# Attention over sixteen batches: the norm, queries, keys and values of batches 4 to 9 computed during batches 0 to 2 and passed through DRAM

## The chip, the cores and the metric

The kernel runs on one core of one Trainium2 chip. The metric is device time in microseconds (us) of one execution, as the median of several. The engines of a core are named as the profile names them: PE (TensorE, matmuls), PEld (the weight loads that run beside PE), DVE (VectorE), ACT (ScalarE), POOL (GpSimd) and SP (SyncE, which here only issues DMAs). Each engine takes its own instructions strictly in order.

## The reference

Two layers, each a conditioning block followed by a feed-forward block, over x of 16 batches x 256 tokens x 256 features, all in float32. Only the last block is touched: attention with 16 heads of 16 features, then a mixture of 8 experts of which each token takes 2.

```python
x = x + _L0_ffn_ref(_L0_cond_ref(x, ...), ...)
y = _L1_cond_ref(x, ...)              # a recurrence over the 256 tokens
x = x + _L1_ffn_ref(y, ...)

def _L1_ffn_ref(x, ln1_g, ln1_b, w_qkv, b_qkv, w_o, b_o, ...):
    h = _layernorm(x, ln1_g, ln1_b)
    q, k, v = jnp.split(h @ w_qkv + b_qkv, 3, axis=-1)
    ...
    scores = jnp.einsum('bqhd,bkhd->bhqk', q, k) / np.sqrt(DK)
    attn = jax.nn.softmax(scores, axis=-1)
    o = jnp.einsum('bhqk,bkhd->bqhd', attn, v).reshape(B, S, D)
    x = x + o @ w_o + b_o
    h = _layernorm(x, ln2_g, ln2_b).reshape(B * S, D)
    topv, topi = jax.lax.top_k(h @ gate_w + gate_b, TOPK)
    ...
    hid = jax.nn.relu(jnp.einsum('td,edf->etf', h, W1) + b1[:, None, :])
    out_e = jnp.einsum('etf,efd->etd', hid, W2) + b2[:, None, :]
    return x + jnp.einsum('etd,te->td', out_e, ew).reshape(B, S, D)
```

What matters for the change: in attention a batch needs nothing from another batch, so the norm, queries, keys and values of any batch can be computed as soon as the recurrence has ended. The experts of a token can be chosen only when attention of its batch has ended.

## The kernel before

The first layer and the recurrence of the second take the time to 2383 us. They leave the recurrence's output, in layout [128 partitions, 2 halves of the features, tokens], in a DRAM tensor `zd`; batch 0 of it also stays on chip in `z0`. The change lies in the stage behind that: attention, batch after batch, with the experts' work interleaved.

Per batch there are three generators, that is functions whose `yield` marks a place where other work may be put between:

- `front(b)` loads z of the batch after (`load_z`), normalizes z of batch b (`normed`: matmuls with a matrix of 1/256 for the mean, L1207, and the variance, L1216; DVE subtracts, takes the reciprocal, scales and shifts, L1209 and L1219 to L1222; POOL squares, L1211; ACT takes the square root, L1218), then makes queries and keys (L1241, evacuated by ACT at L1244 into the tile `qk`) and values (L1252, evacuated by DVE at L1254 into one of two buffers `vbuf`).
- `heads(b)` is the attention itself. For each of four groups of heads (`QC` = 4) it computes the scores once to find each row's largest (L1277, DVE at L1284), moves the queries by it (L1289, L1290), computes the scores again (L1277), takes the exponential (ACT, L1296), and at the end of each half multiplies by the values (L1305, evacuated at L1306 and L1307).
- `ends(b)` divides by the row sums, projects (L1339), adds the residual, normalizes again, picks the experts and scatters each token's row to its expert's place in DRAM (L1330 to L1468).

The experts' work is a fourth generator, `experts()`: for each of 71 tiles of 128 rows it loads rows and weights (L1486 to L1495), transposes (L1501), and does two matrix products, L1513 with W1 and L1526 with W2. W2 of all experts sits in one on-chip tile `mw2` (64 KB a partition, 8 MB in all), loaded by eight DMAs of 1 MB at the start of the stage (L1117).

`drive` puts them together. During batch b it steps through `heads(b)`, and between its places takes steps of `ends(b - 1)`, `front(b + 1)` and the experts. How many tiles belong to a batch follows from how many are certain to be full: none in batches 0 to 2, the first three steps of one (its loads) in batch 3, and then three or four a batch until batch 15 (`allowed`, `planned`). What is left runs alone after attention, from 3341 us.

The text's order is not the engines' order. A scheduler sorts the instructions of each engine by when it expects them to be ready, so work of neighbouring batches overlaps, and a DMA may be issued far ahead of the text. A wait that turns out longer than expected then blocks what stands behind it on that engine.

PSUM, the matmuls' output memory, is full: two buffers of pool `pmm` (handed out by `mm()`, and used by every small product of `front`, `heads` and `ends`), four of `psc` for the scores, two of `pg` for the experts' tiles.

The loop of the stage, with the number of steps that each side work gets in a batch:

```python
steps(front(0))
for b in range(B):
    sides = []
    if b:
        sides.append((ends(b - 1), 9))
    if b + 1 < B:
        sides.append((front(b + 1), 6))
    drive(heads(b), sides, planned(b - 1), planned(b), NPL)
drive(ends(B - 1), [], planned(B - 1), allowed(B - 1), 16)
```

Of the kernel before, what the change touches and what calls it, by code (L numbers as in the profile page):

```python
# [8 lines left out]
F32 = mybir.dt.float32  # L9
# [8 lines left out]
P = 128  # L18
B, T, D = 16, 256, 256
N = B * T  # L20
KC = D // P
E = 8
# [8 lines left out]
AH, DK = 16, 16  # L31
DFF = 1024
NF = DFF // P
# [6 lines left out]
def bc(ap, axis, n):  # L40

    a = ap.unsqueeze(axis)
    shape = list(a.shape)
    shape[axis] = n
    return a.to_broadcast(shape)


def steps(gen, n=None):

    while n is None or n > 0:  # L50
        if next(gen, gen) is gen:
            return
        n = None if n is None else n - 1
# [108 lines left out]
def adaln_ffn_kernel(ctx: ExitStack, tc: tile.TileContext, i: dict, out: bass.AP):  # L162
    nc = tc.nc
# [74 lines left out]
    with (  # L238
# [402 lines left out]
    zd = dram.tile([P, KC, B, T], F32, name="zd")  # L641
    late.close()
    with tc.tile_pool(name="cw", bufs=1) as cw:
# [8 lines left out]
        dram2 = ctx.enter_context(tc.tile_pool(name="dram2", bufs=1, space=DRAM))  # L652
# [7 lines left out]
        QC = AH * 32 // P  # L660
# [18 lines left out]
        with (  # L679
# [276 lines left out]
            def new_w():  # L956
                return cx.tile([P, NC, P], F32, name="wts")
# [6 lines left out]
            early = new_w()  # L964
            w = new_w()
# [37 lines left out]
            g = dt.tile([P, 5, KC * CW], F32, name="g")  # L1003
# [21 lines left out]
            for u in range(NCH + 1):  # L1025
# [20 lines left out]
                for q in range(NQ):  # L1046
                    if u < NCH:
                        steps(dense, 1)
                    if u + 1 < NCH:
# [26 lines left out]
    QC = AH * 32 // P  # L1076
    HC = AH // QC
    QP = QC // 2
    NTT = T // P
    I32 = mybir.dt.int32  # L1080
    final = ctx.enter_context(ExitStack())
    with (
# [5 lines left out]
        fx = attn.enter_context(tc.tile_pool(name="fx", bufs=2))  # L1088
# [5 lines left out]
        zs = {0: z0}  # L1094

        def load_z(b):
            zs[b] = fx.tile([P, KC, T], F32, name="z", bufs=3)
            nc.sync.dma_start(out=zs[b], in_=zd[:, :, b])
# [9 lines left out]
        for m in range(2 * HC):  # L1108
            to, at = slice(m * DK, (m + 1) * DK), slice(m % HC * 32, m % HC * 32 + DK)
# [3 lines left out]
        wg = load("wg", [P, KC, E], fl)  # L1113
        bg = load("bg", [P, E], fl)
        mw2 = ew.tile([P, E, NF, D], F32, name="mw2")
        for e in range(E):
            nc.sync.dma_start(out=mw2[:, e], in_=i["mw2"][:, e])  # L1117

        ones_d = fl.tile([P, P], F32, name="ones_d")
        nc.vector.memset(ones_d, 1.0 / D)  # L1120
# [34 lines left out]
        vbuf = [fl.tile([P, NTT, AH, 32], F32, name=f"v{n}") for n in range(2)]  # L1155
# [41 lines left out]
        now = {"count": count, "full": full, "tiles": tiles}  # L1197
        sent = []

        def mm():  # L1200
            return pmm.tile([P, NTT, T], F32, name="mm", tag="mm")

        def normed(x, which, out):

            mean = mm()[:, 0]
            for k in range(KC):
                nc.tensor.matmul(mean, ones_d, x[:, k], start=(k == 0), stop=(k == KC - 1))  # L1207
            h = fx.tile([P, KC, T], F32, name=f"h{which}", bufs=2 - which)
            nc.vector.tensor_tensor(h, x, bc(mean, 1, KC), ALU.subtract)  # L1209
            sq = fx.tile([P, KC, T], F32, name="sq", bufs=1)  # L1210
            nc.gpsimd.tensor_tensor(sq, h, h, ALU.mult)  # L1211
            out.append(h)
            yield
            var = mm()[:, 0]
            for k in range(KC):
                nc.tensor.matmul(var, ones_d, sq[:, k], start=(k == 0), stop=(k == KC - 1))  # L1216
            rs = fx.tile([P, T], F32, name="rs", bufs=1)
            nc.scalar.activation(rs, var, AF.Sqrt, bias=eps)  # L1218
            nc.vector.reciprocal(rs, rs)  # L1219
            nc.vector.tensor_tensor(h, h, bc(rs, 1, KC), ALU.mult)  # L1220
            for k in range(KC):
                nc.vector.tensor_scalar(  # L1222
                    h[:, k], h[:, k], lnw[:, 2 * which, k : k + 1], lnw[:, 2 * which + 1, k : k + 1], ALU.mult, ALU.add
                )
            yield

        qks, vs, outs = {}, {}, {}

        def front(b):

            if b + 1 < B and b > 0:
                load_z(b + 1)
            o = []
            yield from normed(zs[b], 0, o)
            hn = o[0]
            qk = qks[b] = fx.tile([P, 2, QC, T], F32, name="qk")
            for w in range(2):
                pq = mm()
                for c in range(QP):
                    for k in range(KC):  # L1240
                        nc.tensor.matmul(pq[:, c], wqk[:, w, k, c * P : (c + 1) * P], hn[:, k], start=(k == 0), stop=(k == KC - 1))  # L1241
                for c in range(QP):
                    for r in range(2):
                        nc.scalar.activation(  # L1244
                            qk[:, w, 2 * c + r], pq[:, c], AF.Identity, bias=bias[:, w, c, r : r + 1], scale=keep[:, w, r : r + 1]
                        )
                    yield
            v = vs[b] = vbuf[b % 2]
            pv = mm()
            for t in range(NTT):  # L1250
                for k in range(KC):
                    nc.tensor.matmul(pv[:, t], hn[:, k, t * P : (t + 1) * P], wv[:, k], start=(k == 0), stop=(k == KC - 1))  # L1252
            for t in range(NTT):
                nc.vector.tensor_tensor(  # L1254
                    v[:, t].rearrange("p (m a) (h r) -> p m (a h) r", a=2, h=2)[:, :, 0:4:3],
                    pv[:, t].rearrange("p (m a r) -> p m a r", a=2, r=DK),
                    bv.rearrange("p (m a r) -> p m a r", a=2, r=DK),
                    ALU.add,
                )
            yield  # L1260

        def rows(j):
# [60 lines left out]
        def ends(b):  # L1323
# [20 lines left out]
            yield  # L1344
            o = []
            yield from normed(z, 1, o)
            nc.gpsimd.tensor_tensor(x, x, z, ALU.add)
            nc.scalar.dma_start(out=x3d[:, :, b * T : (b + 1) * T], in_=x)
# [204 lines left out]
        def go(to):  # L1553

            if to > state["gone"]:
                steps(moe, to - state["gone"])
                state["gone"] = to

        def allowed(m):

            return max(0, min(NTL, m * 2 * T // P - E + 1))

        def planned(b):

            return min(allowed(b - 1), 5 + max(0, b - 4) * 40 // 11)

        def drive(main, sides, tiles_from, tiles_to, places):

            a, z = tiles_from * PIECES, tiles_to * PIECES
            for k in range(places):  # L1570
                steps(main, 1)
                for s, n in sides:
                    steps(s, (k + 1) * n // places - k * n // places)
                go(a + (z - a) * (k + 1) // places)
            steps(main)
            for s, _ in sides:
                steps(s)

        NPL = 2 * QC + 1
        steps(front(0))  # L1580
        for b in range(B):
            sides = []
            if b:
                sides.append((ends(b - 1), 9))
            if b + 1 < B:
                sides.append((front(b + 1), 6))
            drive(heads(b), sides, planned(b - 1), planned(b), NPL)
        drive(ends(B - 1), [], planned(B - 1), allowed(B - 1), 16)
        attn.close()
        pools["first"] = final.enter_context(tc.tile_pool(name="ep2", bufs=2, space=PSUM))  # L1590
# [7 lines left out]
        for c in range(NBLK):  # L1598
            t = jx.tile([P, KC, TBLK], F32, name=f"base{c}")
# [93 lines left out]
```

## Time and profile before

| what | us |
|---|---|
| median of 3 runs (3614.8 to 3624.22) | 3615.62 |
| the profiled execution, own time | 3609.16 |
| its span, first to last instruction | 3607.4 |
| recurrence ends (last step's DVE instruction, L951) | 2383.3 |
| front of batch 0 on PE | 2384.0 to 2401.5 |
| heads of batches 0 to 15 | 2401.5 to 3340.6 |
| experts' rest and the output | 3340.6 to 3607.4 |

The end of a batch is taken here as the start of its second copy at L1306, which frees the last product of its heads. These copies start at 2441.0, 2494.3, 2543.2, 2593.0 (batches 0 to 3), 2658.3, 2711.8, 2777.4, 2832.4, 2900.1 (batches 4 to 8), and 2965.0, 3019.1, 3085.1, 3151.4, 3208.2, 3275.6, 3340.6. So batches 1 to 3 take 53.3, 48.9 and 49.8 us, and from batch 4 on a batch takes 53 to 57 us with three tiles of experts and 65 to 68 us with four.

In tables of stretches of time the columns are, for each stretch: its length, then busy us and (instructions) of PE, PEld, DVE, ACT and POOL, the TensorE clock that the throttle granted as a share of full speed, the mean busy share of the 16 DMA engines, and GB/s. In a timeline each line is a group of equal instructions: start, length, engine, line of the kernel, operation, output and inputs, count; in brackets the engine's idle time before it and what ended it. PE records overlap a little, because matmuls are pipelined, so the time that a group holds PE is taken from its start to the start of the next.

### The profile page before, as it was taken

The numbers are of one execution on the slowest core, as the hardware profiler recorded it, in microseconds if no ns is written. First come the engines' busy times: TensorE is split into PE (matmuls) and PEld (weight loads), VectorE is DVE, ScalarE is ACT, GpSimd is POOL, SyncE is SP. The second block draws the span as 40 slices with busy tenths as digits, with TensorE's granted clock in tenths as the row PEclk, the third lists the DMA queues.
The fourth block names the chain that finished last, engine by engine and source line by source line (L and its number), as shares of the span: only waits on it lengthen the run. The fifth ranks groups of instructions, "written<-read, shape, count | busy, mean of one in ns | idle before, by whom it ended". The sixth has DMA issues, their size and how long they took to land.

```text
span 3607.4 us, 72831 instructions
## 1 busy us (share of the span) xinstructions
PE 3373.3 (94%) x26776; PEld 2564.6 (71%) x26776; DVE 2277.7 (63%) x7358; ACT 1492.2 (41%) x3701; POOL 686.0 (19%) x1164
## 2 busy tenths in 40 slices
PE   8899969999999999999999999969999999999896
PEld 4377456777777777777777777735677777777796
DVE  3333477988788887878788787435555556564323
ACT  1133135555454544545454554334444434443221
POOL 4545220000000100000010100101222222222221
PEclk9999989999999999999999999968999999999997
DMA  6333441011111111011111111130223333332566
GB/s 213 125 108 104 146 73 29 18 36 22 36 19 33 24 35 33 20 36 22 36 19 33 28 28 31 24 123 21 70 92 114 104 119 103 117 102 97 195 216 222
DMA packets 422255, 272.78 MB, mean 76 GB/s; under 512 B 304720, under 2 KB 381136, under 8 KB 411024
## 3 DMA queue, kind: packets, MB, share of 16 engines
q1 hardware_dynamic: 397504, 207.95, 20.9%
q0 software_dynamic: 13344, 36.60, 2.7%
q10 hardware_dynamic: 11056, 23.60, 1.9%
q8 instruction: 216, 3.54, 0.4%
q14 instruction: 135, 1.11, 0.1%
HBM read 191.62 MB, written 76.44 MB: 74 GB/s over the span
## 4 chain that ended last, share of the span: by engine, by line
PE 73%; DVE 10%; issue 5%; DMA 4%; ACT 4%; POOL 2%; SPq 1%; ACTq 0%; DVEq 0%; POOLq 0%
PE acc L865 13%; PE po L839 9%; PE gp L933 7%; PE wp L822 7%; PE g L1526 6%; PE g L1513 5%; PE sc L1277 3%; PE bp L889 3%; PE sp L736 3%; PE ph L529 2%; PE mm L1305 2%; PE py L543 2%; DVE i L747 2%; DVE s L746 1%; PE mm L1241 1%
## 5 line engine op out<-in xcount | busy, mean ns | idle before, releaser
L839 PEld LDWEIGHTS po<-yt,kin 128*128 128x128 f32 x3840 | 459.1, 191 | 104.4 <-issue 103.5
L865 PEld LDWEIGHTS acc<-ge,kout 128*128 128x128 f32 x3968 | 467.0, 192 | 86.1 <-issue 42.4
L865 PE MATMUL acc<-ge,kout 128*128 128x128 f32 x3968 | 505.5, 280 | 3.2 <-DVE ge L862 1.7
L839 PE MATMUL po<-yt,kin 128*128 128x128 f32 x3840 | 507.0, 281 | 0.0
L826 ACT COPY wts<-wp 64x256 f32<-64x256 f32 x1024 | 374.4, 366 | 181.1 <-PE wp L822 168.2
L952 POOL TENSOR_SCALAR zt<-hT 128x32 f32<-128x32 f32 x256 | 122.3, 478 | 1553.9 <-DVE hT L951 1434.6
L933 PE MATMUL gp<-wh,hT 128*32 128x256 f32 x4096 | 318.3, 393 | 30.5 <-DVE hT L951 21.4
L817 DVE TENSOR_TENSOR oh<-chosen,parted 128x1024 f32<-128x1024 f32 x256 | 311.9, 1218 | 0.0
L822 PE MATMUL wp<-oh,ol 128*64 128x128 f32 x4096 | 297.3, 281 | 5.7 <-ACT wts L826 5.1
L1517 ACT ACTIVATE hT<-g,b 128x128 f32<-128x128 f32 x284 | 104.4, 368 | 426.3 <-DVE hT L1519 365.0
L1526 PE MATMUL g<-mw,hT 128*128 x1136 | 273.3, 396 | 5.8 <-ACT xT L1503 3.1
L1513 PE MATMUL g<-xT,w 128*128 128x128 f32 x2272 | 274.3, 276 | 1.1 <-DVE ys L1531 1.1
L1513 PEld LDWEIGHTS g<-xT,w 128*128 128x128 f32 x2272 | 269.0, 192 | 5.7 <-DVE ys L1531 1.3
L822 PEld LDWEIGHTS wp<-oh,ol 128*64 128x64 f32 x4096 | 226.5, 137 | 57.6 <-issue 12.8
L1526 PEld LDWEIGHTS g<-mw,hT 128*128 128x128 f32 x1136 | 221.3, 200 | 42.3 <-ACT xT L1503 8.1
L843 ACT ACTIVATE ge<-po 128x512 f32<-128x512 f32 x248 | 147.1, 593 | 202.6 <-PE po L839 195.2
L933 PEld LDWEIGHTS gp<-wh,hT 128*32 128x32 f32 x4096 | 118.8, 110 | 155.0 <-issue 49.0
L814 DVE TENSOR_TENSOR ol<-chosen,iota 128x512 f32<-128x512 f32 x256 | 175.0, 683 | 66.9 <-ACT chosen L798 47.3
L939 ACT ACTIVATE g<-gp 128x192 f32<-128x192 f32 x256 | 84.5, 330 | 287.4 <-PE gp L933 286.0
L1277 PE MATMUL sc<-qk 32*128 32x256 f32 x2048 | 193.7, 416 | 9.0 <-DVE npads L1284 7.2
L862 DVE TENSOR_TENSOR ge<-ge,wts 128x512 f32<-128x512 f32 x248 | 169.3, 683 | 38.8 <-ACT ge L843 30.0
L1519 DVE TENSOR_SCALAR hT<-g,b 128x128 f32<-128x128 f32 x284 | 96.9, 342 | 134.6 <-PE g L1513 71.2
(354 smaller groups left out, 5395.6 us busy)
## 6 DMA issues: line engine op xcount, KB each, us to landing
w<-in_mw SPq DMA_DIRECT2D x71, 1024.0 KB
xwd<-xw SPq DMA_DIRECT2D x64, 256.0 KB
xr<-xwd SPq DMA_DIRECT2D x256, 64.0 KB
xs<-axd SPq DMA_DIRECT2D x71, 129.0 KB
xs<-xsd SPq DMA_DIRECT2D x71, 129.0 KB
b<-in_b SPq DMA_DIRECT2D x71, 128.0 KB
r<-ayd SPq DMA_DIRECT2D x64, 128.0 KB
mw<-in_mw SPq DMA_DIRECT2D x8, 1024.0 KB
```

Of the source, the lines that this page charges most:

```text
L814: nc.vector.tensor_tensor(ol, bc(c[:, 0, g : g + GT], 2, NK), bc(iota[:, 0:NK], 1, GT), ALU.is_equal)
L817: nc.vector.tensor_tensor(oh, bc(c[:, 1, g : g + GT], 2, P), bc(parted, 1, GT), ALU.is_equal)
L822: nc.tensor.matmul(wp[half[s], t], ol[:, at, :], oh[:, at, :], start=True, stop=True)
L826: nc.scalar.copy(wr[half[h], :, :, at : at + GH], wp[half[s], :, :, h * NHI : (h + 1) * NHI].rearrange("p t r c -> p c r t"))
L839: nc.tensor.matmul(po[:, h, :].rearrange("p (b t) -> p b t", t=SPC), kin[:, k, (c + h) * P : (c + h + 1) * P], yu[:, k], start=(k == 0), s ...
L843: nc.scalar.activation(to, po, AF.Gelu)
L862: nc.vector.tensor_tensor(ge, ge, w[:, c : c + CQ, :], ALU.mult)
L865: nc.tensor.matmul(acc[d], kout[:, c + h, d * P : (d + 1) * P], ge[:, h, :], start=(c + h == 0), stop=(c + h == NC - 1))
L933: nc.tensor.matmul(gp[j * CW : (j + 1) * CW], state["hT"][:, k, :], group(wh, k, j), start=False, stop=(k == KC - 1), skip_group_check=True,)
L1277: nc.tensor.matmul(s[j][:, t], qk[rows(j), w, c, t * P : (t + 1) * P], qk[rows(j), 1 - w, c, :], start=True, stop=True)
L1513: nc.tensor.matmul(ph[:, f], w1[n][:, k, at * P : (at + 1) * P], xT[n][:, k], start=(k == 0), stop=(k == KC - 1))
L1526: m = nc.tensor.matmul(acc, hT[n][:, f], mw2[:, bass.ds(e, 1), f].rearrange("p o d -> p (o d)"), start=(f == 0), stop=(f == NF - 1))
```

## The change

`front` gets a second form, `front(b, n)`, which computes the same for batch b = 4 + n into slots that lie inside `mw2`: four slots of 3584 floats a partition (queries and keys, values, z), and three work tiles and one small one for the norm. When it is done, two DMAs write queries and keys (1 MB) and values (0.5 MB) to DRAM tensors `qkd` and `vd`. The new generator `made_ahead` runs it for batches 4 to 9; each batch 0 to 2 takes 12 of its steps (a front has 7), and what is left runs at the start of batch 3.

During batches 3 to 8, `front(b + 1)` is replaced by `fetch(b + 1)`, which loads z of the batch after, and queries, keys and values of batch b + 1, and computes nothing. Fronts 0 to 3 and 10 to 15 stay as they were.

The eight loads of `mw2` move from the start of the stage to batch 3, after `made_ahead` has ended; each waits for the slots that it overwrites. Four fills of the slots' value parts (128 x 1024 each) are new on POOL.

As long as `early["on"]` holds (to the start of batch 3), `mm()` hands out buffers of `pmm` and of `pg` in turn, so that small products have four PSUM buffers and not two.

```diff
         mw2 = ew.tile([P, E, NF, D], F32, name="mw2")
-        for e in range(E):
-            nc.sync.dma_start(out=mw2[:, e], in_=i["mw2"][:, e])
+        EARLY, AHEAD, SLOTS = 4, range(4, 10), 4
+        QKN, VN, ZN = 2 * QC * T, NTT * AH * 32, KC * T
+        room = mw2.rearrange("p e f d -> p (e f d)")
+        slots = []
+        for n in range(SLOTS):
+            at = n * (QKN + VN + ZN)
+            slots.append((room[:, at : at + QKN], room[:, at + QKN : at + QKN + VN], room[:, at + QKN + VN : at + QKN + VN + ZN]))
+            nc.gpsimd.memset(slots[n][1], 1.0)
...
+        qkd = dram2.tile([len(AHEAD), P, QKN], F32, name="qkd")
+        vd = dram2.tile([len(AHEAD), P, VN], F32, name="vd")
...
+        early = {"on": True, "n": 0}
         def mm():
+            early["n"] += 1
+            if early["on"] and early["n"] % 2:
+                t = pg.tile([P, NF // 2, P], F32, name="g", tag="g")
+                return t.rearrange("p f n -> p (f n)").rearrange("p (t n) -> p t n", t=NTT)
             return pmm.tile([P, NTT, T], F32, name="mm", tag="mm")
...
+        def fetch(b):
+            if b + 1 < B:
+                load_z(b + 1)
+            n = AHEAD.index(b)
+            qks[b] = fx.tile([P, 2, QC, T], F32, name="qk")
+            nc.sync.dma_start(out=qks[b].rearrange("p w c t -> p (w c t)"), in_=qkd[n])
+            vs[b] = vbuf[b % 2]
+            nc.sync.dma_start(out=vs[b].rearrange("p t h r -> p (t h r)"), in_=vd[n])
+            yield
...
-        def front(b):
+        def front(b, ahead=None):
...
+                slot = slots[ahead % SLOTS]
+                z = slot[2].rearrange("p (k t) -> p k t", t=T)
+                nc.sync.dma_start(out=z, in_=zd[:, :, b])
+                yield from normed(z, 0, o, ahead)
...
+            if ahead is not None:
+                nc.sync.dma_start(out=qkd[ahead], in_=slot[0])
+                nc.sync.dma_start(out=vd[ahead], in_=slot[1])
             yield
...
+        def made_ahead():
+            for n, b in enumerate(AHEAD):
+                yield from front(b, n)
         steps(front(0))
+        made = made_ahead()
         for b in range(B):
             sides = []
             if b:
                 sides.append((ends(b - 1), 9))
             if b + 1 < B:
-                sides.append((front(b + 1), 6))
+                sides.append((fetch(b + 1), 1) if b + 1 in AHEAD else (front(b + 1), 6))
+            if b < EARLY - 1:
+                sides.append((made, 6 * len(AHEAD) // (EARLY - 1)))
+            elif b == EARLY - 1:
+                steps(made)
+                early["on"] = False
+                for e in range(E):
+                    nc.sync.dma_start(out=mw2[:, e], in_=i["mw2"][:, e])
             drive(heads(b), sides, planned(b - 1), planned(b), NPL)
```

More of the change, by code (lines that the diff above doesn't have):

```diff
@@ L1115, in adaln_ffn_kernel @@
         mw2 = ew.tile([P, E, NF, D], F32, name="mw2")
-        for e in range(E):
-            nc.sync.dma_start(out=mw2[:, e], in_=i["mw2"][:, e])
+        EARLY, AHEAD, SLOTS = 4, range(4, 10), 4
[6 more added lines that the diff above has]
+            nc.gpsimd.memset(slots[n][1], 1.0)
+        free = SLOTS * (QKN + VN + ZN)
+        own = [room[:, free + n * ZN : free + (n + 1) * ZN].rearrange("p (k t) -> p k t", t=T) for n in range(3)]
+        own_rs = room[:, free + 3 * ZN : free + 3 * ZN + T]
+        qkd = dram2.tile([len(AHEAD), P, QKN], F32, name="qkd")
+        vd = dram2.tile([len(AHEAD), P, VN], F32, name="vd")
         ones_d = fl.tile([P, P], F32, name="ones_d")
@@ L1198, in adaln_ffn_kernel, with normed @@
         sent = []
+        early = {"on": True, "n": 0}
         def mm():
+            early["n"] += 1
+            if early["on"] and early["n"] % 2:
+                t = pg.tile([P, NF // 2, P], F32, name="g", tag="g")
+                return t.rearrange("p f n -> p (f n)").rearrange("p (t n) -> p t n", t=NTT)
             return pmm.tile([P, NTT, T], F32, name="mm", tag="mm")
-        def normed(x, which, out):
+        def normed(x, which, out, ahead=None):
             mean = mm()[:, 0]
@@ L1207, in normed @@
                 nc.tensor.matmul(mean, ones_d, x[:, k], start=(k == 0), stop=(k == KC - 1))
-            h = fx.tile([P, KC, T], F32, name=f"h{which}", bufs=2 - which)
+            h = fx.tile([P, KC, T], F32, name=f"h{which}", bufs=2 - which) if ahead is None else own[ahead % 2]
             nc.vector.tensor_tensor(h, x, bc(mean, 1, KC), ALU.subtract)
-            sq = fx.tile([P, KC, T], F32, name="sq", bufs=1)
+            sq = fx.tile([P, KC, T], F32, name="sq", bufs=1) if ahead is None else own[2]
             nc.gpsimd.tensor_tensor(sq, h, h, ALU.mult)
@@ L1216, in normed @@
                 nc.tensor.matmul(var, ones_d, sq[:, k], start=(k == 0), stop=(k == KC - 1))
-            rs = fx.tile([P, T], F32, name="rs", bufs=1)
+            rs = fx.tile([P, T], F32, name="rs", bufs=1) if ahead is None else own_rs
             nc.scalar.activation(rs, var, AF.Sqrt, bias=eps)
@@ L1227, in adaln_ffn_kernel @@
         qks, vs, outs = {}, {}, {}
-        def front(b):
-            if b + 1 < B and b > 0:
+        def fetch(b):
+            if b + 1 < B:
                 load_z(b + 1)
-            o = []
-            yield from normed(zs[b], 0, o)
+            n = AHEAD.index(b)
[5 more added lines that the diff above has]
+        def front(b, ahead=None):
+            o = []
+            if ahead is None:
+                if b + 1 < B and b > 0:
+                    load_z(b + 1)
+                yield from normed(zs[b], 0, o)
+                qk = qks[b] = fx.tile([P, 2, QC, T], F32, name="qk")
+                v = vs[b] = vbuf[b % 2]
+            else:
+                slot = slots[ahead % SLOTS]
+                z = slot[2].rearrange("p (k t) -> p k t", t=T)
+                nc.sync.dma_start(out=z, in_=zd[:, :, b])
+                yield from normed(z, 0, o, ahead)
+                qk = slot[0].rearrange("p (w c t) -> p w c t", w=2, c=QC)
+                v = slot[1].rearrange("p (t h r) -> p t h r", t=NTT, h=AH)
             hn = o[0]
-            qk = qks[b] = fx.tile([P, 2, QC, T], F32, name="qk")
             for w in range(2):
@@ L1247, in front @@
                     yield
-            v = vs[b] = vbuf[b % 2]
             pv = mm()
@@ L1576, in drive @@
             for s, _ in sides:
-                steps(s)
+                if s is not made:
+                    steps(s)
         NPL = 2 * QC + 1
+        def made_ahead():
+            for n, b in enumerate(AHEAD):
+                yield from front(b, n)
         steps(front(0))
+        made = made_ahead()
         for b in range(B):
```

## The prediction

> **What bounds the kernel now.** I read the engines' totals first, then the chain that ended last, then the stretches batch by batch, because the change touches only some 500 us of the span and an average over all of it says little there.
>
> ```profile
> PE 3373.3 (94%) x26776; PEld 2564.6 (71%) x26776; DVE 2277.7 (63%) x7358; ACT 1492.2 (41%) x3701; POOL 686.0 (19%) x1164
> ...
> PE 73%; DVE 10%; issue 5%; DMA 4%; ACT 4%; POOL 2%; SPq 1%; ACTq 0%; DVEq 0%; POOLq 0%
> ```
>
> PE bounds the whole. The stretches of batches 0 to 5, each ended by its second copy at L1306, show that this isn't equally true of every batch:
>
> ```profile
> 2401.50:2441.00 39.50, 34.47 (x226) 20.63 (x225) 16.58 (x28) 17.89 (x31) 1.04 (x1) 0.83 0.28 112
> 2441.00:2494.30 53.30, 49.39 (x285) 31.64 (x285) 29.00 (x73) 21.06 (x37) 9.87 (x17) 0.81 0.06 20
> 2494.30:2543.20 48.90, 44.59 (x285) 28.77 (x285) 28.94 (x73) 21.09 (x37) 9.84 (x17) 0.90 0.09 28
> 2543.20:2593.00 49.80, 45.57 (x303) 30.71 (x303) 29.15 (x76) 21.74 (x40) 10.87 (x18) 0.90 0.16 54
> 2593.00:2658.30 65.30, 60.77 (x462) 48.15 (x466) 34.85 (x95) 26.70 (x55) 16.58 (x24) 0.97 0.36 123
> 2658.30:2711.80 53.50, 51.86 (x427) 41.70 (x424) 33.37 (x90) 25.53 (x54) 14.70 (x22) 1.00 0.28 90
> ```
>
> From batch 4 on PE is busy 93 to 97% at a granted clock of 0.97 to 1.00. In batches 0 to 3 the clock is 0.81 to 0.90, weight loads cover only 52 to 62%, and PE waits for others: heads alternate between PE, 16 reductions a batch on DVE (L1284, 681 ns) and 16 exponentials on ACT (L1296, 604 ns). How much PE has to spare shows between batches 3 and 5: batch 5 holds three more tiles of experts, and is only 53.5 - 49.8 = 3.7 us longer. A tile holds PE for 7.4 us (below), so 22.3 us of PE went in for 3.7.
>
> **What is removed.** The timeline of PE in batch 8, at nearly full clock, gives the price of a front. Starts to the next starts:
>
> ```profile
> 2842.18 1.13 PE L1207 MATMUL mm<-z,ones_d 128*128 128x256 f32 x4
> 2843.14 1.95 PE L1513 MATMUL g<-xT,w 128*128 128x128 f32 x16
> ...
> 2860.59 1.13 PE L1216 MATMUL mm<-sq,ones_d 128*128 128x256 f32 x4
> 2861.55 1.89 PE L1241 MATMUL mm<-h,wqk 128*128 128x256 f32 x8
> 2863.28 1.95 PE L1513 MATMUL g<-xT,w 128*128 128x128 f32 x16
> ```
>
> L1207 holds PE 0.96 us, L1216 0.96, L1241 1.73 and comes twice, L1252 (2898.78 to 2900.70) 1.92: a front is **7.3 us of PE**. A tile is two L1513 groups at 1.88 and L1526 at 3.67, together 7.4. Batches 4 to 8 lose a front each. In the 65 us batches (4, 6, 8) PE has no room, so 7.3 each. Batches 5 and 7 (53.5 and 55.0) might be held near 49 us by the chain of heads, and then lose only about 5 each; but the front also leaves that chain, on DVE and ACT (below), and 2 of the 4 table loads of a batch at 1283 ns go too. I take 7.3: 5 x 7.3 = **-36.6**, its other end 3 x 7.3 + 2 x 5 = -32. In the order in which the scheduler puts the changed kernel's instructions batch 3 gives up its own front (for batch 4) and gets the last made one, for batch 9: equal work, and some of it before its heads start, **-1**.
>
> **What is added.** That order has two made fronts in batch 0, one in 1, two in 2. Each is 7.3 us of PE (8.6 at a clock of 0.85); on DVE L1209 677 + L1219 1749 + L1220 689 + 2 x L1222 408 + 2 x L1254 417 = 4.8 us; on ACT 8 x L1244 564 + L1218 473 + a table load or two = 5.6 to 7.5; POOL 1.0. The trace of before has no second front in a batch, so I bound its cost:
> - below: the tiles' slope, 3.7 us for 22.3 of PE, 0.17 each; a front on PE 1.2, and about 0.9 more since it has per us of PE twice the DVE and ACT work of a tile: 2.1. It could even be negative if the clock rises by more work (next part).
> - above: what `ends` costs. Batches 1 and 2 have it and batch 0 doesn't: 9.4 to 13.8 us more for 9.5 us of PE and 12 of DVE. By its share, a front of 7.3 and 4.8: 6.4. Nothing hidden at all, at clock 0.85: 8.6.
>
> I take **3.5**, nearer to the tiles: like them a front depends on nothing in heads, and the diff gives small products four PSUM buffers for this stretch, so neither side waits so often for a copy. 5 x 3.5 = **+17.5** (10 to 32).
>
> **A rule against the clock.** The row: L1241 x8 shows 2.88 us in batch 1 (2468.20) (granted clock 0.81) and 1.89 in batch 8 (0.95 over the batch). The Trainium skill, "TensorE: Matmul & The Clock Gate", § What's actually happening, says that the default is throttled and activity releases it. By the row alone a moved front costs 8.6 of PE time and buys nothing. By the rule, filling gaps lifts the clock for the batch's own 45 us: at 0.90 to 1.00 up to 4.5 us in each of batches 2 and 3, at 0.81 more in 1. Batches 4 and 5 agree with it, batch 1 (93% busy, lowest clock) doesn't. I count nothing for it in the sum, and let it carry the lower end.
>
> **A rule about room.** By PE busy, batch 2 has 48.9 - 44.6 = 4.3 us left, less than a front. The skill's "Perfetto Trace Analysis", § Identifying the Most-Contended Engine, says that matmul busy misjudges headroom and weight-load busy is the measure: 28.8 of 48.9 is 59%, against 78% in batch 5, a room of 9.3 us where a front's weight loads take 32 x some 0.2 = 6.5, so 1.4 fronts a batch fit. By the first, five fronts would cost 5 x 7.3 less 3 x 4.3, about 24; by the second next to nothing. The pair 3 and 5 sides with the second.
>
> **What moves at no cost, and its cover.**
> - The 8 MB of `mw2` (L1117) left SP from 2389.20 and took some 22 us at 412 to 426 GB/s. Now the last three loads go behind the stores of front 9, about 15 us into batch 3, and land about 35 us into it. The first user, the second product of the first tile (L1526 before), stands in the middle of batch 4, some 12 us in: about 25 us of slack.
> - Six times 1.5 MB written and read back, at those rates 4 us a piece; after the store of the last z (L1068, issued at 2383.73 in 0.58 us) the load that waits for it (L1098) could go at 2388.48, 4.2 us later. Here batches lie between, and DMA stands at 6 to 36% busy. A fetch is issued a batch ahead; values wait for their buffer, and the tile loads queue behind on SP, which in batch 3 of before waited for the end of the batch too.
> - Seven z loads of 256 KB at the stage's start share the queues with nothing of `mw2` any more.
> - Four POOL fills of 0.95 us wait for the store of `zd`, and POOL's next work is later.
>
> **Sum**: -36.6 - 1 + 17.5 = -20.1. The profiled execution took 3609.2, 6.5 below the median, so 3589.1 of its kind and **3596** on the median's scale.
>
> **Rivals.** A measurement tells some 0.3%, 10.8 us, so faster is below 3604.8 and slower above 3626.5.
> - A, as above, 3581 to 3605 (0.6 to 5.4 us a front): chance 0.43.
> - D, wholly hidden and the clock rises: -37.6 and 4 us of the own work of batches 0 to 3, **3574**: 0.12. For it the pair 3 and 5, against it batch 1.
> - S, each front costs its share by `ends`, 6.4: -37.6 + 32 = -5.6, **3610**: 0.12.
> - B, the slower one: the made fronts' DVE and ACT work lands on the alternation of reductions and exponentials, because both engines work in order and a reciprocal of 1.75 us or a table load stands in front of a copy that PE waits for. 4.8 + 5.6 = 10.4 us a front, 5 x 10.4 = 52: 52 - 37.6 = +14.4, **3630**. It decides from 7.5 us of lengthening a front (+ 37.6 / 5), and is slower in the sense above from 9.7. For it: DVE's idle time before L1219 is ended by ACT (75.1 of 75.2 us over 32), and `ends` cost more than its PE time in batch 1. Against it: DVE is busy 42 to 59% and ACT 40 to 45% in these batches: 0.27.
> - C, a late `mw2`: if its last loads slip by a whole batch, 50 - 25 = 25 us of PE waiting in batch 4, -20 + 25, **3621**: 0.06.
>
> That the change does not do what it says is part of S: batches 4 to 8 could be bound by heads and not shorten.
>
> Faster is A and D, 0.55; same S and C, 0.18; slower B, 0.27. A's own range is 3581 to 3605; the range for 8 in 10 goes from D, 3574, to a little past B, 3632.
>
> **What will show it.** Batch 4 to 8 between their copies should be 7 us shorter each (65 to 58, 53.5 to 46 or 48); if 5 and 7 lose under 4, heads bound them. Batches 0, 1 and 2 should be 46, 57 and 56 us; past 60 for batch 0 or 2 it is B, and then DVE's or ACT's line ends PE's waits before the scores and the copies. The granted clock in 0 to 3 tells D. The second product of the first tile must not wait for `mw2`, nor scores of batch 4 for `qk`. I am wrong above all if a made front lengthens its batch by over 7.5 us.

## The result: 46 us slower

The changed kernel takes 3661.6 us (median of 6 runs, 3656.17 to 3666.72) against 3615.21 (3611.22 to 3624.25): ratio 1.0129, 95% interval 1.0113 to 1.0144. Forecast were 3596 and a range up to 3632. The profiled execution took 3661.24, its span is 3658.5.

Lines move by the edit: L1207 is L1226 now, L1211 is L1230, L1216 is L1235, L1241 is L1280, L1277 is L1318, L1306 is L1347, L1355 is L1396, L1486 is L1527, L1526 is L1567. First the engines' totals and the chain that ended last:

```profile
PE 3395.2 (93%) x26776; PEld 2583.5 (71%) x26776; DVE 2280.6 (62%) x7358; ACT 1485.0 (41%) x3695; POOL 690.7 (19%) x1168
...
PE 70%; DVE 10%; DMA 7%; issue 5%; ACT 4%; POOL 3%; SPq 1%; ACTq 0%; DVEq 0%; POOLq 0%
```

PE executes exactly as many instructions as before; in the chain DMA has gone from 4% to 7% and PE from 73% to 70%. The stretches of batches 0 to 5, each ended by its second copy at L1347 (columns as before):

```profile
2403.00:2450.08 47.08, 42.28 (x284) 27.83 (x284) 24.32 (x40) 29.50 (x52) 3.12 (x3) 0.89 0.13 46
2450.08:2519.48 69.40, 55.79 (x336) 37.98 (x336) 36.12 (x84) 26.98 (x49) 11.94 (x19) 0.83 0.21 76
2519.48:2579.69 60.21, 52.28 (x345) 38.68 (x346) 35.91 (x86) 29.92 (x55) 11.96 (x19) 0.91 0.33 121
2579.69:2638.18 58.49, 52.63 (x314) 36.61 (x315) 29.82 (x77) 21.68 (x41) 9.48 (x15) 0.80 0.54 184
2638.18:2705.20 67.02, 58.37 (x418) 45.51 (x422) 30.84 (x87) 19.79 (x43) 14.89 (x24) 0.85 0.37 123
2705.20:2763.19 57.99, 51.66 (x406) 40.61 (x406) 29.90 (x84) 18.72 (x41) 14.81 (x22) 0.94 0.37 125
```

| stretch | before | changed | difference |
|---|---|---|---|
| 2384 to the end of batch 0 | 57.0 | 66.1 | +9.1 |
| batch 1 | 53.3 | 69.4 | +16.1 |
| batch 2 | 48.9 | 60.2 | +11.3 |
| batch 3 | 49.8 | 58.5 | +8.7 |
| batches 4 to 8 | 307.1 | 312.0 | +4.9 |
| batches 9 to 15 | 440.5 | 440.9 | +0.4 |
| rest | 266.8 | 267.5 | +0.7 |

Both terms of the sum failed. Batches 0 to 3 got 45 us longer instead of 17. The two profiled executions differ by 51 us and the medians by 46, and part of the 45 can be spread between executions: batches 1 and 2 hold the same work in the kernel mw2_late (below), and take 116.0 us in its profile where they take 102.2 in that of before. Batches 4 to 8, freed of a front each, got no shorter: in batch 4 the granted clock is now 0.85 (it was 0.97), and in batch 5 DMA moves 125 GB/s instead of 90 and PE is busy 89% (51.66 of 57.99) instead of 97%. From batch 3 to batch 8 no wait of PE is put down to a DMA, so neither the late `mw2` nor a late `qk` held the matmuls up directly.

### The profile page after: what moved, and what is told of

Read it like the earlier page. It is cut to its first block, busy times and chain, and to the rows that moved or that the text cites. A ratio compares the mean times of both kernels' runs of the same rounds, so it can differ in the third digit from the quotient of the medians.

```text
span 3658.5 us, 72931 instructions
## 1 busy us (share of the span) xinstructions
PE 3395.2 (93%) x26776; PEld 2583.5 (71%) x26776; DVE 2280.6 (62%) x7358; ACT 1485.0 (41%) x3695; POOL 690.7 (19%) x1168
## 4 chain that ended last, share of the span: by engine, by line
PE 70%; DVE 10%; DMA 7%; issue 5%; ACT 4%; POOL 3%; SPq 1%; ACTq 0%; DVEq 0%; POOLq 0%
PE acc L865 13%; PE po L839 9%; PE gp L933 7%; PE wp L822 6%; PE g L1567 6%; PE g L1554 5%; PE bp L889 3%; PE sp L736 3%; PE sc L1318 3%; PE ph L529 2%; PE py L543 2%; DMA axd<-row,slot 2%; DVE i L747 2%; DVE s L746 1%; PE mm L1346 1%
## 5 line engine op out<-in xcount | busy, mean ns | idle before, releaser
L1554 PE MATMUL g<-xT,w 128*128 128x128 f32 x2272 | 281.9, 280 | 1.9 <-DVE ys L1572 1.9
L1567 PE MATMUL g<-mw,hT 128*128 x1136 | 273.8, 396 | 8.1 <-ACT xT L1544 5.2
L822 PEld LDWEIGHTS wp<-oh,ol 128*64 128x64 f32 x4096 | 225.8, 137 | 56.9 <-issue 13.5
L1567 PEld LDWEIGHTS g<-mw,hT 128*128 128x128 f32 x1136 | 221.4, 200 | 45.3 <-ACT xT L1544 10.6
L1318 PE MATMUL sc<-qk 32*128 32x256 f32 x2048 | 193.8, 415 | 15.4 <-DVE npads L1325 13.8
```

The costliest lines, as they stand in the source:

```text
L822: nc.tensor.matmul(wp[half[s], t], ol[:, at, :], oh[:, at, :], start=True, stop=True)
L1318: nc.tensor.matmul(s[j][:, t], qk[rows(j), w, c, t * P : (t + 1) * P], qk[rows(j), 1 - w, c, :], start=True, stop=True)
L1554: nc.tensor.matmul(ph[:, f], w1[n][:, k, at * P : (at + 1) * P], xT[n][:, k], start=(k == 0), stop=(k == KC - 1))
L1567: m = nc.tensor.matmul(acc, hT[n][:, f], mw2[:, bass.ds(e, 1), f].rearrange("p o d -> p (o d)"), start=(f == 0), stop=(f == NF - 1))
```

## What ate the gain of batches 4 to 8

**Accounting on PE.** I summed PE's timeline over these five batches, each group from its start to the start of the next, waits apart. Before: work 293.5 us, waits 13.5. Changed: 282.4 and 29.6. The fronts' groups did go: L1241 17.3, L1252 10.8, half of L1207 and L1216 5.0 and 4.3, together 37.4, close to the 36.6 of the forecast. But the remaining groups, nearly equal in number, hold PE 26.3 us longer, and the waits grew by 16.1. The largest waits of PE in batches 4 to 8, first of before, then of the changed kernel (total, times, longest):

```profile
PE mm L1355 <- ACT hT L1517: 6.3, 5, 1.7
```

```profile
PE mm L1396 <- DVE h L1241: 16.0, 5, 3.7
PE mm L1330 <- DVE npads L1325: 3.9, 3, 1.5
PE mm L1380 <- POOL odd L1375: 3.7, 2, 2.8
```

The logits of `ends` (L1355, now L1396) wait for the norm: table load, square root, reciprocal, two scalings. Fronts used to stand in that time. Without them PE waits there some 3 us in each of the five batches, 16.0 us in all where it was 6.3.

**Experiment no_fronts**: the removal alone. In the kernel before:

```diff
-                sides.append((front(b + 1), 6))
+                sides.append((skipped(b + 1), 1) if 4 <= b + 1 < 10 else (front(b + 1), 6))
```

`skipped` loads z as before, fills queries and keys on POOL and leaves the values' buffer as it is.

> The kernel before with the fronts of batches 4 to 9 left out (queries and keys filled on POOL, the values of an earlier batch), so that the output differs; nothing is made ahead, nothing is fetched, the experts' second weights are loaded at the start as before. It measures what the removal alone is worth. By the prediction's term 6 fronts of 7.3 us are 44 us less, 3572. If heads bound these batches, the gain is under 15 us, 3600 or more.

Measured 3611.48, ratio 0.999 (0.9974 to 1.0007). Ratios, with their 95% intervals, are to runs of the kernel before beside each experiment; its median was 3616 to 3621 on these occasions. Six fronts less, 44 us of PE, are worth between 9 us and nothing. Batches 4 and 5 of it, and PE's timeline in batch 5:

```profile
2610.15:2677.15 67.00, 57.31 (x430) 44.48 (x430) 31.11 (x88) 19.55 (x43) 19.66 (x29) 0.87 0.35 115
2677.15:2729.15 52.00, 47.92 (x386) 38.11 (x387) 30.14 (x83) 18.69 (x43) 15.49 (x22) 0.97 0.30 100
```

```profile
2703.38 0.49 PE L1522 MATMUL g<-xT,w 128*128 128x128 f32 x2
2706.57 0.36 PE L1364 MATMUL mm<-w_wg,h 128*128 128x8 f32 x2 [2.69 <-DVE h L1222]
...
2708.46 2.77 PE L1522 MATMUL g<-xT,w 128*128 128x128 f32 x14
```

A wait of 2.69 us, and just behind it fourteen matmuls of the experts (L1522, L1513 of before) take 2.77 us, where sixteen took 1.95 in the rows shown with the forecast. The granted clock was 0.67 and then 0.60 behind this wait:

```profile
2706.57:2708.46 1.89, 1.89 (x12) 1.89 (x13) 1.89 (x5) 0.00 (x0) 0.00 (x0) 0.67 0.00 0
2708.46:2711.16 2.70, 2.70 (x15) 2.58 (x15) 1.23 (x6) 0.37 (x1) 0.00 (x0) 0.60 0.00 0
```

At this place the gap is paid twice: once as a wait, once by the slower clock after it. Summed as above, batches 4 to 8 of this kernel have 37.4 us of fronts less, other groups 17.8 longer (L1277, the scores, alone 47.9 to 57.3), waits 13.8 longer. As an estimate, the clock can account for 12 of the 17.8 at most: what it lacked of full speed, times the length of each stretch, adds up to some 19 us in these five batches and to 7 in those of before.

**Experiments before_short and no_fronts_short**: the square root and the reciprocal out of the norm in `ends`, with and without the fronts.

```diff
+            if which:
+                rs = var
+            else:
+                rs = fx.tile([P, T], F32, name="rs", bufs=1)
+                nc.scalar.activation(rs, var, AF.Sqrt, bias=eps)
+                nc.vector.reciprocal(rs, rs)
```

> The kernel before, all fronts in place, with the square root and the reciprocal left out of the norm in ends, so that the output differs. Theory gap: PE waits only some 9 us for that norm in batches 4 to 8 because fronts fill the time, so 5 to 20 us less than before over all sixteen batches, about 3600. Rival, heads bound the batches: the DVE and ACT time that goes (about 4.8 us a batch) shortens every batch, 40 us or more.

> The kernel before without the fronts of batches 4 to 9, and with the square root and the reciprocal left out of the norm in ends (the rows are multiplied by the variance itself), so that the output differs. Theory gap: without the fronts PE has nothing to do while the logits of ends wait for that norm (15.7 of 27.3 us of PE's waits in batches 4 to 8), and the clock falls behind each gap; that ate the 36 us of the removed fronts. With the chain some 3.5 us shorter the waits go, and this kernel is 20 us or more below the same shortening of the kernel with its fronts (label before_short). Rival, heads bound these batches: within 8 us of before_short.

Measured 3564.72 (0.9851, 0.9833 to 0.9868) and 3545.3 (0.9794, 0.978 to 0.9808). The pair came out nearly as the theory of the gap says: once the chain is short, the missing fronts are worth 19.4 us, just under the 20 it asked. The first kernel by itself was a miss for me: 55 us less, where I expected about 15. That number fits the rival on record, that heads bound every batch (40 us or more), but its places don't: from batch 4 on the batches with three tiles shortened by 0.4 to 1.3 us in the profiles, and those with four by 2.7 to 6.8. So the norm's chain ends late also where fronts fill PE, and most where a batch holds four tiles. Batch 5 of each:

```profile
2650.38:2703.22 52.84, 51.64 (x427) 41.52 (x420) 31.82 (x89) 22.85 (x51) 15.03 (x23) 1.00 0.28 91
```

```profile
2654.73:2702.51 47.78, 46.09 (x386) 36.45 (x386) 28.45 (x82) 15.98 (x39) 15.68 (x22) 1.00 0.33 109
```

With fronts (first line) 52.8, without 47.8, both at full clock: five of the 7.3 us now show. Of the batches with four tiles, batch 6 shows nothing yet (61.3 and 62.0) and batch 8 shows 3.4 us (61.6 and 58.2); the chain that ended last in batch 6 without fronts ends in the scatter of rows, the tile's row load and DVE.

This pair also shows that much of what made the other groups longer is not the clock. Without fronts they are 16.8 us longer here too, of which the clock, reckoned as above, can account for 7 at most (9 against 2); the scores alone hold PE 58.4 us instead of 47.6. One group of them in batch 8, where the granted clock was 1.00 (L1289 and L1296 are L1277 and L1284 of before):

```profile
2822.19 2.56 PE L1289 MATMUL sc<-qk 32*128 32x256 f32 x16
2823.03 0.29 PEld L1289 LDWEIGHTS sc<-qk 32*128 32x128 f32 x2 [0.31 <-DVE npads L1296]
2823.63 0.72 PEld L1289 LDWEIGHTS sc<-qk 32*128 32x128 f32 x10 [0.30 <-DVE npads L1296]
```

Sixteen of these matmuls take 1.15 us in the whole groups of batch 8 of before_short. Here their weight loads wait inside the group for DVE's reductions, which free the scores' buffers, and PE counts as busy meanwhile. Waits of this kind add up to 1.8 us in batches 4 to 8 of before, 3.8 in no_fronts and 6.7 in the changed kernel. So the alternation of heads between PE and DVE, which PE's busy time hides, is part of what came back; what the rest is due to stays open.

**Experiment no_fronts_tiles**, beside **before_tiles**: is the room on PE usable by more tiles?

```diff
-            return min(allowed(b - 1), 5 + max(0, b - 4) * 40 // 11)
+            return min(allowed(b - 1), 5 + max(0, b - 4) * 4)
```

> The kernel before without the fronts of batches 4 to 9 (output differs), and with four tiles planned in every batch from 4 on, 49 by the end of attention instead of 45. Theory gap: the time of PE that the fronts leave is usable only by other work that is ready; a tile put there costs a few us, and one fewer at the end saves about 10 (266 us for 26 tiles and the output), so 3580 to 3600, below 3611. Rival, heads bound these batches and a tile costs what it always does: 3605 to 3615.

> The kernel before with four tiles planned in every batch from 4 on, nothing else. Both theories: PE is full in batches with fronts, a tile costs its 7.4 us or more there and saves about 10 at the end, so within 12 us of before. It stands beside no_fronts_tiles.

Measured 3631.09 (1.0025, 1.0009 to 1.0041) and 3628.32 (1.0019, 1.0008 to 1.003). A miss for the theory, and above the range of its rival: a fourth tile in a batch without a front costs more than it saves at the end. Batches 4 to 8 with four tiles take 64 to 66 us with a front and 64 to 67 without.

**Experiment no_fronts_xpool**: the residual's load, which holds the next tile's row load behind it on SP, on POOL's queue.

```diff
-            nc.sync.dma_start(out=x, in_=x1d[:, :, b])
+            nc.gpsimd.dma_start(out=x, in_=x1d[:, :, b])
```

> The kernel before without the fronts of batches 4 to 9 (output differs), and the load of the residual in ends (x from x1d), which on SP waits for the store of the batch before and holds the next tile's row load behind it, on POOL's queue instead. Theory: after the fronts are gone it is the experts' feed through SP that bounds batches with four tiles, 10 to 20 us less than no_fronts. Rival, the wait of the logits for the norm alone bounds them: within 5 us of no_fronts.

Measured 3621.47, ratio 1.0 (0.9984 to 1.0017), the same as no_fronts: that load is not what binds. What binds a batch of four tiles without a front, beyond the norm, stays open.

**Experiment no_fetch**: the changed kernel without the fetch's two loads.

```diff
-            nc.sync.dma_start(out=qks[b].rearrange("p w c t -> p (w c t)"), in_=qkd[n])
+            nc.gpsimd.memset(qks[b], 0.01)
             vs[b] = vbuf[b % 2]
-            nc.sync.dma_start(out=vs[b].rearrange("p t h r -> p (t h r)"), in_=vd[n])
```

> The changed kernel without the two loads of queries, keys and values in the fetch (a fill on POOL stands for queries and keys, the values of an earlier batch stay in the buffer), so that the output differs; the stores are left in. Theory transfers: the 1.5 MB of a fetch stand in front of the tiles' row loads, DVE waits 5.6 us for such a load at batch ends, and that eats what the removed fronts save: batches 4 to 8 shorten by 25 to 37 us together, time near 3630. Rival, heads bound batches 4 to 8 whatever PE has to do: they stay as long as now, 3655 to 3662. Second rival, the lower clock of these batches eats it: they stay as long as now too, with the clock at 0.85 to 0.95.

Measured 3649.21 (1.0085, 1.0055 to 1.0115): 12 us less than the changed kernel, and still far above the 3630 of the theory, which gave the fetch the whole loss. One thing that the transfers can do shows on SP's queue at the end of batch 6 of the changed kernel, and on DVE after it:

```profile
2822.61 0.33 SPq L1532 DMA_DIRECT2D w<-in_mw  x1
...
2824.16 0.62 SPq L1254 DMA_DIRECT2D qk<-qkd  x1
2826.72 0.34 SPq L1527 DMA_DIRECT2D xs<-xsd  x1
```

```profile
2833.27 0.15 DVE L1574 COPY to<-xs 128x1 uint32<-128x1 uint32 x1 [5.58 <-DMA xs<-xsd]
2833.34 0.48 DVE L1374 SCALAR_TENSOR_TENSOR odd<-oT,other,odd 128x256 f32<-128x256 f32 x1
2833.74 2.48 DVE L1325 TENSOR_REDUCE npads<-sc 128x2 f32<-128x512 f32 x4
```

The row load `xs`, issued at 2826.72 with 1 MB of queries and keys and 1 MB of weights just ahead of it, lets DVE go on only at 2833.27, 6.5 us later; the same place of before took from 2774.40 to 2776.71, 2.3 us:

```profile
2774.40 0.34 SPq L1486 DMA_DIRECT2D xs<-xsd  x1
2776.71 0.15 DVE L1533 COPY to<-xs 128x1 uint32<-128x1 uint32 x1 [1.55 <-DMA xs<-xsd]
```

The instruction that waits is a copy of one number a row, but the reductions that free the scores stand behind it on DVE. Yet this one load doesn't explain the 12 us. All of DVE's waits for row loads in batches 4 to 8, in before, the changed kernel and no_fetch:

```profile
DVE to L1533 <- DMA xs<-xsd: 40.2, 11, 6.8
DVE to L1574 <- DMA xs<-xsd: 34.8, 13, 5.8
DVE to L1573 <- DMA xs<-xsd: 33.2, 12, 3.6
```

They are not longer than before. That the fetch costs something is shown; by which wait is not. In the profile of no_fetch batches 4 to 8 are 5.5 us shorter than in the changed kernel, where the theory asked for 25 to 37.

## What made batches 0 to 3 longer

**Experiment sq_on_dve.** POOL's timeline at the end of batch 1 of the changed kernel, and what PE and DVE did then:

```profile
2505.99 0.96 POOL L1455 DMA_INDIRECT xsd<-row,slot  x1 [0.30 <-issue]
2506.94 0.32 POOL L1436 COPY row<-dest_i 128x1 int32<-128x1 int32 x2
2512.41 0.30 POOL L1436 COPY row<-dest_i 128x1 int32<-128x1 int32 x2 [5.16 <-DMA xsd<-row,slot]
2512.67 1.04 POOL L1230 TENSOR_TENSOR mw<-mw 128x512 f32<-128x512 f32 x1
```

```profile
2513.76 2.08 PE L1235 MATMUL g<-mw,ones_d 128*128 128x256 f32 x4 [6.36 <-POOL mw L1230]
```

```profile
2516.38 1.75 DVE L1238 RECIPROCAL mw<-mw 128x256 f32<-128x256 f32 x1 [8.48 <-ACT mw L1237]
```

After the scatter POOL's next instruction is a small copy into the same row buffer for the next batch. It waits until the scatter has landed, and the made front's square waits behind it; PE then waits for the square, DVE for PE. So:

```diff
-            nc.gpsimd.tensor_tensor(sq, h, h, ALU.mult)
+            (nc.gpsimd if ahead is None else nc.vector).tensor_tensor(sq, h, h, ALU.mult)
```

> The changed kernel with the square of the made fronts (L1230) on DVE instead of POOL. Theory POOL queue: in batch 1 of the changed kernel the made front's square stood on POOL behind a copy (L1436) that waited 5.16 us for the scatter of rows, and PE then waited 6.36 us for it; without that, batches 1 and 2 shorten by some 5 us each and the time is near 3650. Rival, the alternation of DVE and ACT work with PE in the heads: the square only moves 0.7 us a front to the busier engine, and the time stays at 3660 or rises by 2 to 4 us.

Measured 3648.37 (1.0093, 1.0064 to 1.0121): 13 us less, as the theory of POOL's queue says. Batch 1 went from 69.4 to 58.0; batch 2 did not shorten (62.5), so it was one wait rather than one a batch.

**Experiment mw2_late**: the eight loads alone moved to batch 3 in the kernel before.

```diff
+            if b == 3:
+                for e in range(E):
+                    nc.sync.dma_start(out=mw2[:, e], in_=i["mw2"][:, e])
```

> The kernel before with one part of the change alone: the eight 1 MB loads of the experts' second weights moved from the start of the stage to batch 3. By the prediction nothing changes, within 3 us of 3615. By the theory that these 8 MB hold up the first tiles' row loads and the scatter's descriptors in batches 3 and 4, 3 to 9 us more, in batches 3 and 4.

Measured 3616.46, ratio 1.001 (0.999 to 1.003). This part costs nothing, as forecast.

**Experiment made_alone**: sq_on_dve and no_fetch together.

> The changed kernel with the square of the made fronts on DVE and without the two loads of the fetch (queries and keys filled on POOL, values of an earlier batch, so that the output differs). What is left of the change is six fronts made beside batches 0 to 2, their stores, the late second weights, and batches 4 to 8 without fronts. If POOL's queue and the transfers are separate causes, their savings (13 and 12 us) add up: about 3637, and against no_fronts (3611) some 24 us or 4 us a made front remain, near the 3.5 that the prediction took. Rival, all three are one cause (too much work in batches 0 to 3): 3646 to 3650, no less than with either alone.

Measured 3643.33 (1.0076, 1.0061 to 1.0092), between the two expectations: the savings overlap (18 us instead of 25), and against no_fronts (0.999) 0.0086 x 3616 = 31 us are left for making six fronts and storing them, 5.2 each.

**Experiments pe_fill and dve_act_fill** take a made front apart. Both start from mw2_late and put six times either the matmuls of a front (fixed inputs, no reader) or its DVE and ACT work (buffers of its own) where the made fronts were:

```diff
+            if b < 3:
+                sides.append((filler, 12))
             if b == 3:
+                steps(filler)
```

> The kernel mw2_late (the second weights loaded in batch 3) with the matmuls of six fronts, on fixed inputs and read by nobody, in the places where the changed kernel has the made fronts: some 44 us of PE work at full clock and nothing on DVE, ACT or POOL. Theory room: PE has only 25 us of waits in batches 0 to 3, most of them too short for a front, so 15 to 30 us more than mw2_late (3616). Rival, the DVE and ACT work is what costs: within 6 us of mw2_late. Third, the filled gaps lift the clock (two batches at a granted clock of 0.74 took 58.0 us each, at 0.90 48.9): no longer, or shorter by up to 15 us.

> The kernel mw2_late with the DVE and ACT work of six fronts (subtract, square, square root with its table loads, reciprocal, scale, eight copies to queries and keys, two to values), on buffers of its own, in the same places, and none of their matmuls: some 5.5 us of DVE and 6 to 7 us of ACT a front. Theory room: hidden, within 6 us of mw2_late. Rival, this work lands on the alternation of reductions and exponentials: 15 to 35 us more, with longer waits of PE for the reductions (L1284 of the kernel before).

Measured 3640.9 (1.0051, 1.0035 to 1.0068) and 3627.44 (1.0016, 0.9995 to 1.0037). Less mw2_late's 0.001, the matmuls cost 15 us by ratios (21 by medians), the DVE and ACT work 2 (7 by medians): the theory of room, not the alternation. Of made_alone's 31 us this leaves 3 to 14 for the stores and for the two kinds of work being one chain, which no run took apart; pe_fill also has two PSUM buffers for small products, where the changed kernel has four. Batches 1 and 2 of mw2_late, then of pe_fill:

```profile
2446.60:2504.58 57.98, 54.29 (x285) 34.27 (x286) 28.96 (x73) 20.86 (x38) 9.91 (x17) 0.74 0.06 19
2504.58:2562.57 57.99, 54.27 (x285) 34.16 (x285) 28.95 (x73) 20.84 (x37) 9.85 (x17) 0.74 0.07 24
```

```profile
2442.03:2501.05 59.02, 53.81 (x341) 37.58 (x342) 28.98 (x73) 20.97 (x38) 9.88 (x17) 0.91 0.06 18
2501.05:2559.47 58.42, 53.60 (x337) 36.73 (x338) 29.29 (x74) 20.84 (x37) 9.85 (x17) 0.91 0.10 29
```

These two executions differ by some 55 matmuls a batch and by 0.4 to 1.0 us: with the added work the clock was 0.91 and not 0.74. But mw2_late's batches 1 and 2 hold the same instructions as those of before, which took 53.3 and 48.9 at 0.81 and 0.90 in the profile shown. Against that execution the matmuls cost 6 to 10 us a batch.

## A version faster than both

The late chain is the norm, so **before_rsqrt** shortens it in the kernel before, and **after_rsqrt** in sq_on_dve:

```diff
-            nc.scalar.activation(rs, var, AF.Sqrt, bias=eps)
-            nc.vector.reciprocal(rs, rs)
+            nc.scalar.activation(rs, var, AF.Abs_reciprocal_sqrt, bias=eps)
```

> The kernel before with the reciprocal square root on ACT in one instruction instead of a square root on ACT and a reciprocal on DVE (1749 ns), in all norms of the stage. The chain that the logits of ends wait for is 1.75 us shorter, half of what before_short took out (3.5 us, 55 us of time): 20 to 40 us less than before. If only the table loads counted in before_short, which stay here: within 8 us of before.

> The changed kernel with the square of the made fronts on DVE and the reciprocal square root on ACT in one instruction. Theory gap: with the chain shorter, batches without fronts gain somewhat more than those with fronts (no_fronts_short was 19 us below before_short), so 25 to 50 us below sq_on_dve (3648), about 3610, still above before_rsqrt by 15 to 30 us.

Measured 3585.96 (0.9915, 0.99 to 0.9929) and 3600.73 (0.9956, 0.9939 to 0.9973). ACT's instruction takes as long as the square root did (474 ns), so one reciprocal of 1749 ns a norm is gone, and with it 30 us. Neither leaves out any of the computation, and both are faster than the kernel before; after_rsqrt is some 10 us below the 3610 expected of it. The change itself costs 15 us also here, half of the 32 it costs in sq_on_dve; the missing fronts are worth more once the chain is shorter, as in the pair above, but no run shows that this is all of the difference.

## Why the prediction failed, by its steps

- **"Batches 4 to 8 lose a front each ... 5 x 7.3 = -36.6"** failed. The 7.3 us a front was right (37.4 us of groups went), its worth wasn't: all six together are worth between 9 us and nothing in no_fronts, since waits grew by 13.8 us and the other groups by 17.8. "PE has no room" was read from PE busy at 93 to 97%, but the fronts were what filled PE while the norm's chain ran. The forecast had considered a floor for batches 5 and 7 alone, and put the case that these batches don't shorten under S, at 0.12, with a time of 3610; I looked for what limits the batch with the front in it and never asked what PE waits for once it is out.
- **"I take 3.5, nearer to the tiles: 5 x 3.5 = +17.5"** failed: made_alone has 31 us for six, 5.2 each, inside its bounds of 2.1 and 6.4, and the whole change 45. The slope of 0.17 between batches 3 and 5 set a batch at a clock of 0.90 against one at 1.00, so part of its room was clock; that a tile can also stand beside other chains than a front is my reading, which no run shows.
- **What was costed at nothing**: the late second weights, rightly. The fetch wrongly: 12 us alone, 5 with the square moved (sq_on_dve to made_alone), by a wait that stays open. Wrongly also the square: I priced POOL's 1.0 us and named the queue for the fills, but not for the square behind the scatter: 13 us.
- **The clock rule.** The forecast let the Trainium skill's "TensorE: Matmul & The Clock Gate", § What's actually happening, by which activity releases the throttle, count only for the batches that gained work. It counts against those that lost it: among the profiles with the norm as before, batch 4 has a granted clock of 0.97 in the five where it makes a front, and of 0.83 to 0.88 in the seven where it doesn't. For the gain in batches 0 to 2 the profiles agree less firmly: batches 1 and 2 have 0.73 to 0.93 in seven profiles without added matmuls, and 0.83 to 0.94 in five with them. The clock returned 12 us of the 37 in no_fronts at most; no run held it fixed.
- **The rule about room.** "By the first, five fronts would cost ... about 24; by the second next to nothing." Six fronts' matmuls cost 15 to 21, so PE busy was the nearer measure here. The skill's "Perfetto Trace Analysis", § Identifying the Most-Contended Engine, names the share of peak arithmetic beside weight-load busy; the forecast used weight-load busy alone, and sided with it by the pair of batches 3 and 5.
- **Rival B** gave the right sign and 3630, by the wrong mechanism: DVE and ACT work alone is worth 2 to 7 us. Its ACT term is also off as written: 8 x 564 + 473 ns and one or two table loads of 1283 are 6.3 to 7.6 us and not 5.6 to 7.5, which would put B at 3634.

The parts, from separate runs: removal -4, matmuls +15 to 21, DVE and ACT +2 to 7, POOL's queue +13, fetch +5 to 12, together 31 to 49 of the 46. They overlap, so the split is not exact, and the four PSUM buffers and the stores have no run of their own.

## What to carry to other kernels

Before work is taken out of a busy engine, ask what that engine will wait for when it is gone: work that fills the time of a chain can be nearly free, and removing it shows the chain. Leave the work out altogether for one run; that told in one step that no more than 9 us could be won here by any way of making fronts earlier, as long as the norm's chain stays. And an elementwise instruction that costs little by itself, as POOL's square of 1.0 us, is priced by what it stands behind and what waits for it.

## What the runs showed of the chip

The same 285 matmuls of a batch without tiles took 48.9, 53.3 or 58.0 us, at granted clocks of 0.90, 0.81 and 0.74: 53.3 and 48.9 in batches 1 and 2 of before, 48.9 and 53.3 in those of before_tiles, 57.98 and 57.99 in those of mw2_late. So one profile of before gives the length of such a batch no better than by some 9 us, and the kernels that have these batches spread widely (3603.7 to 3637.0 in 23 runs of the kernel before beside pe_fill). The kernels with a shorter chain show less of it, but in four and five runs only (before_short 3561.88 to 3568.72, before_rsqrt 3584.49 to 3589.15).
